# A spectral convolution with its mix of channels: the block-diagonal operand is loaded from DRAM instead of being spread on the engines

## The chip, the cores and the metric

The kernel runs on one core of a Trainium2 chip. The metric is the device time of one execution in microseconds, the median of three runs: 6919.16 us (6918.71 to 6933.95). The profile comes from one further execution with the profiler on.

A core has engines with queues of their own: PE (TensorE, matmuls; "PEld" is its loading of weights), DVE (VectorE), ACT (ScalarE), POOL (GpSimd) and SP (SyncE, which here only issues DMAs). They meet in semaphores. Data lies in SBUF (128 partitions), in PSUM (where matmuls write) and in DRAM. Sixteen DMA engines move data between DRAM and SBUF.

## The reference, cut to what matters

The input is `x[16, 16, 256, 256]` in float32 (batch, channel, y, x). Two layers follow one another, each on the group-normalised input and added to it. The change lies in the first, a Laplace-domain convolution:

```python
alpha = fft2(x)                                            # [b, i, o, x]
A  = 1 / (omega1[:, None, None, None] - weights_pole1)     # [o, i, k, p]
Bm = 1 / (omega2[:, None, None, None] - weights_pole2)     # [x, i, k, q]
S  = einsum('ikpq,oikp,xikq->oxik', weights_residue, A, Bm)
output_residue1 = einsum('biox,oxik->bkox', alpha, S)      # the mix
x1 = ifft2(output_residue1).real
# ... and a second term from the poles, x2; the layer adds x1 + x2/(256*256)
```

The **mix** is the second `einsum`: at each frequency (o, x) the 16 complex input channels `i` of each of 16 images are multiplied by a complex 16 x 16 matrix `S[o, x]`. The second layer (3 x 3 convolutions, an involution, a gate over channels) takes the greater part of the time and isn't touched.

## The kernel before

`forward` runs four parts one after another: `layer0_forward` (norm, Fourier transform, terms of the poles), `layer0_mix` (the mix and the inverse transform along x), `layer0_back` (inverse transform along y, sum, norm) and `layer1`. They hand over in DRAM: `layer0_forward` writes the spectrum to `al[33, 2, 64, 16, 256]`, with the indices group of four frequencies in y; real or imaginary part `v`; four frequencies `f` of the group times 16 channels; image; frequency in x. `layer0_mix` reads it and writes `hd`.

`layer0_mix` loops over 33 groups `g` of four frequencies in y (the last group has one that is used). For each group:

- `poles` (DVE) spreads the factors `A` of the group over a block-diagonal operand `lt`, three multiplies with the mask `m16`. The factors come by `load_poles` (line 579) into `av`, which has two buffers.
- `residues(lt, s, k0)`, called for k0 = 0, 2, ..., 14, builds the matrices `S` of the group: 16 matmuls with 32 columns of weights each (line 656) into PSUM, copied to `s[128, 256, 2, 16]` by ACT (line 667) or DVE (line 665).
- `mix(s, y, between)` does the multiplication: for each of 256 frequencies in x one matmul (line 679) with `s[:, i]` as weights (128 rows: four frequencies in y, times 16 channels, times real and imaginary; 32 columns) and `alb[:, i]` as the moving operand: 64 columns, that is 4 frequencies in y by 16 images. So that one matmul keeps the four frequencies apart, `alb` is block-diagonal: in column (j, b) only the 32 rows that belong to frequency j are not zero. Four matmuls in a row go to four different column groups of PE (`32 * q`). Sixteen of such fours fill a PSUM tile, and ACT copies it to `y` (line 686); there are four such quarters.
- `turn(y, f)` transposes on PE (line 695) and copies to `yt` by DVE (701) and ACT (699); `columns(g, f, yt)` does the inverse transform along x on PE (714), adds and subtracts on DVE (726, 727), and POOL issues four writes to `hd` (734). The `columns` of f = 3 runs in two halves between the quarters of the next mix (`between`).

The block-diagonal operand is made in two steps. `load_spectrum(g, q)` (SP, line 607) loads the images 4q to 4q + 3 of a group into `alc` (four buffers of 4 KB a partition) with four DMAs, one for each h, each of 128 KB; 16 for a group. `expand(t, q, j, eng)` then multiplies the tile by column j of the mask `m4` (one for rows of frequency j, zero elsewhere) and writes all of block j for these images: on ACT line 617, on DVE line 619. There are 16 such spreads a group, 6 on ACT and 10 on DVE, in the order of the table `spreads`.

The order of PE, ACT, DVE and POOL is written out by hand (`manual_schedule`); SP's is left to the scheduler. After `mix(g)` come residues for the next group, turn and columns for f = 0, 1, 2, a part of the spreads with each f, then the last spread, the last residues and turn for f = 3, and then `mix(g + 1)`. `alb` (64 KB a partition), `s`, `lt` and `y` have one buffer each. The spectrum that is spread in group g has been loaded during group g - 1.

The sides of a DMA have shapes that matter below. `load_spectrum` reads a pattern of 8 blocks x 4 rows x 1,024 words and writes 32 partitions x 1,024 words.

Of the kernel before, what the change touches and what calls it, by code (L numbers as in the profile page):

```python
# [10 lines left out]
F32 = mybir.dt.float32  # L11
I32 = mybir.dt.int32
AF = mybir.ActivationFunctionType
ALU = mybir.AluOpType
# [5 lines left out]
N = 256  # L20
G = 8
P = 128
NF = 33
# [33 lines left out]
def load(nc, pool, src, shape, name):  # L57
    t = pool.tile(shape, F32, tag=name, name=name)
    nc.sync.dma_start(out=t, in_=src)
    return t  # L60
# [505 lines left out]
def layer0_mix(ctx, tc, d, al, hd, tabs):  # L566
# [3 lines left out]
    nc = tc.nc  # L570
    nb = d["x"].shape[0]
    cp = ctx.enter_context(tc.tile_pool(name="mc", bufs=1))
    m16 = load(nc, cp, d["m16"], [P, 4], "m16")
# [3 lines left out]
    def load_poles(g):  # L577
        av = ap.tile([P, 32, 4, 3], F32, tag="av", name="av")
        nc.sync.dma_start(out=av.rearrange("p k f l -> p (k f l)"), in_=avd[g])
        return av  # L580

    av = load_poles(0)
# [6 lines left out]

    alb = cp.tile([P, N, 4, nb], F32, name="alb")
    m4 = load(nc, cp, d["m4"], [P, 4], "m4")

    lp = ctx.enter_context(tc.tile_pool(name="ml", bufs=1))
    gp = ctx.enter_context(tc.tile_pool(name="mg", bufs=1))
# [2 lines left out]
    pst = ctx.enter_context(tc.tile_pool(name="pst", bufs=2, space=PSUM))  # L599
    psh = ctx.enter_context(tc.tile_pool(name="psh", bufs=2, space=PSUM))  # L600

    def load_spectrum(g, q):

        t = gp.tile([P, 4, 2, P], F32, tag="alc", name="alc", bufs=4)
        src = al[g].rearrange("v (j h c) b x -> h (v j) c (b x)", h=4, c=4)
        for h in range(4):
            nc.sync.dma_start(
                out=t[32 * h : 32 * h + 32].rearrange("p b e x -> p (b e x)"),
                in_=src[h, :, :, 4 * q * N : 4 * q * N + 4 * N],
            )  # L610
        return t

    def expand(t, q, j, eng):

        dst = alb.rearrange("p (x e) j b -> p b e x j", e=2)[:, 4 * q : 4 * q + 4, :, :, j]
        if eng is nc.scalar:
            eng.activation(dst, t, AF.Copy, scale=m4[:, j : j + 1])
        else:
            eng.tensor_scalar(dst, t, m4[:, j : j + 1], None, ALU.mult)  # L619


    spreads = (
        (((0, 0), (1, 0)), ((0, 1), (0, 2), (0, 3))),
        (((1, 1), (2, 0)), ((1, 2), (1, 3), (2, 1))),
        (((3, 0), (3, 1)), ((2, 2), (2, 3), (3, 2))),
        ((), ((3, 3),)),
    )

    def spread(spectrum, f):
        for eng, parts in zip((nc.scalar, nc.vector), spreads[f]):  # L630
            for q, j in parts:
                expand(spectrum[q], q, j, eng)

    def poles(av):


        lt = lp.tile([P, 32, 3, 4, 4], F32, tag="lt", name="lt")
        shape = [P, 32, 4, 4]
        for plane in range(3):
            nc.vector.tensor_tensor(  # L640
                lt[:, :, plane],
                av[:, :, :, plane].unsqueeze(3).to_broadcast(shape),
                m16.unsqueeze(1).unsqueeze(2).to_broadcast(shape),
                ALU.mult,
            )
        return lt.rearrange("p (k g) l f c -> p k g l f c", g=4)

    def residues(lt, s, k0):

        kk = k0 // 2  # L650
        ps = psg.tile([P, 2, 2, N], F32, tag="pg", name="ps")
        for v in range(2):
            for g in range(4):
                for odd in range(2):
                    lanes = slice(64 * odd, 64 * odd + 64)
                    nc.tensor.matmul(
                        ps[32 * g : 32 * g + 32, odd, v],
                        lhsT=lt[lanes, kk, g, 1 - v : 3 - v].rearrange("p l f c -> p (l f c)"),
                        rhs=tt[lanes, kk, g],
                        start=True,  # L660
                        stop=True,
                    )
        dst, src = s[:, :, :, k0 : k0 + 2], ps.rearrange("p k v x -> p x v k")
        if kk % 2:
            nc.vector.tensor_copy(dst, src)
        else:
            nc.scalar.copy(dst, src)  # L667

    def mix(s, y, between):


        for x0 in range(0, 64, 16):
            if x0 >= 32:
                next(between, None)
            ps = psg.tile([P, 16, 64], F32, tag="pg", name="pg")
            for x in range(16):
                for q in range(4):
                    i = 4 * (x0 + x) + q
                    nc.tensor.matmul(  # L679
                        ps[32 * q : 32 * q + 32, x],  # L680
                        lhsT=s[:, i].rearrange("p v k -> p (v k)"),
                        rhs=alb[:, i].rearrange("p j b -> p (j b)"),
                        start=True,
                        stop=True,
                    )
            nc.scalar.copy(y[:, :, x0 : x0 + 16], ps.rearrange("p x j -> p j x"))

    def turn(y, f):

        yt = hp.tile([P, 8, 8, C], F32, tag="yt", name="yt", bufs=2)  # L690
        for t0 in range(0, 8, 4):
            pt = pst.tile([P, 4, P], F32, tag="pt", name="pt")
            for t in range(4):
                j = 16 * f + 2 * (t0 + t)
                nc.tensor.transpose(pt[:, t], y[:, j : j + 2].rearrange("p q x -> p (q x)"), ident)
            dst = yt[:, :, t0 : t0 + 4].rearrange("p c t k -> p t c k")
            src = pt.rearrange("p t (c k) -> p t c k", k=C)
            if t0:
                nc.scalar.copy(dst, src)
            else:  # L700
                nc.vector.tensor_copy(dst, src)  # L701
        return yt
# [35 lines left out]

    E = mybir.EngineType
    with tc.manual_schedule(engines={E.PE, E.Activation, E.DVE, E.Pool}):  # L740
        spectrum = [load_spectrum(0, q) for q in range(4)]
        lt = poles(av)
        av = load_poles(1)
        s = gp.tile([P, N, 2, C], F32, tag="s", name="s")
        for k0 in range(0, C, 2):
            residues(lt, s, k0)
        for q in range(4):
            spread(spectrum, q)
        for q in range(4):
            spectrum[q] = load_spectrum(1, q)  # L750
        between = iter(())
        for g in range(NF):
            more = g + 1 < NF
            y = gp.tile([P, 64, 64], F32, tag="y", name="y")
            if more:
                lt = poles(av)
            mix(s, y, between)
            if more:
                s = gp.tile([P, N, 2, C], F32, tag="s", name="s")
                residues(lt, s, 0)  # L760
            for f in range(4 if more else 1):
                if more and f == 3:
                    spread(spectrum, f)
                    for k0 in (12, 14):
                        residues(lt, s, k0)
                yt = turn(y, f)
                if more:
                    for k0 in range(2 if f == 0 else 4 * f, 4 * f + 4, 2) if f < 3 else ():
                        residues(lt, s, k0)
                    if f < 3:  # L770
                        spread(spectrum, f)
                    if g + 2 < NF:
                        if f == 0:
                            av = load_poles(g + 2)
                        spectrum[f] = load_spectrum(g + 2, f)
                between = columns(g, f, yt)
                if f < 3:
                    for _ in between:
                        pass
# [642 lines left out]
def fourier_tables():  # L1422

    k = np.arange(N)
# [3 lines left out]
    def parities(a):  # L1428
        return a.reshape(P, 2, *a.shape[1:])
# [12 lines left out]
        axis=1,  # L1442
# [13 lines left out]
    for t in tt:  # L1456
        for i in ii:
            mt[t, i, :, i // 4, t, i % 4] = 1
    out = {
        "fy": fy.reshape(P, 2, P),  # L1460
        "wx": parities(wx),
        "wxa": parities(wx[..., :P]),
        "wxn": wxn,
        "ix": ix,

        "iy": iy[..., :P].reshape(64, 2, 2, P).transpose(2, 0, 1, 3).reshape(P, 2, P),
        "ones": np.full((P, P), 1.0 / P),
# [7 lines left out]
        "sign_m": np.tile(np.repeat([-1.0, 1.0], 16), 4)[:, None],  # L1475
        "cm": np.tile(np.repeat(np.eye(2), 32, axis=0), (2, 1)),
        "mk": np.tile(np.repeat(np.eye(C), M, axis=0), (2, 1)),
        "m4": np.tile(np.repeat(np.eye(4), 4, axis=0), (8, 1)),
        "m16": np.tile(np.repeat(np.eye(4), M, axis=0), (8, 1)),
        "mt": mt.reshape(P, 4, 8),  # L1480
        "phase": np.repeat([0.25, 0.0], 64)[:, None],
# [73 lines left out]
```

## Time and profile before

| | us |
|---|---|
| median of 3 runs | 6919.16 |
| lowest, highest | 6918.71, 6933.95 |
| profiled execution, its own time | 6939.37 |
| its span, first to last instruction | 6937.6 |

| engine | busy us | share of the span |
|---|---|---|
| PE | 6375.2 | 92% |
| PEld | 3583.2 | 52% |
| DVE | 5451.1 | 79% |
| ACT | 3703.9 | 53% |
| POOL | 3635.8 | 52% |

A line of a group names the line of the kernel, the engine, the operation, the tile written and the tiles read, shapes and count; after the first bar stand busy time in us and the mean of one in ns, and after the second the idle time of the engine just before, with what ended it ("<-"). "issue" is waiting for nothing that the profile shows. In the timeline a line begins with start and length in us. In the tables of windows each engine's busy time stands with its count of instructions in brackets, then the granted clock of PE (1 is full), the mean busy share of the DMA engines and GB/s. Float32 matmuls are listed as two instructions each, so a mix of 256 matmuls shows 512. A matmul's own duration includes its way through the array; many overlap.

### The profile page before, as it was taken

Reading aid. Unit: us, or ns where it says so; the run is one execution under the profiler, and the core shown is the slowest. Engines: PE = TensorE matmul, PEld = TensorE weight load, DVE = VectorE, ACT = ScalarE, POOL = GpSimd, SP = SyncE. Lnnn points to the kernel's source line nnn. Section 1 sums busy time; section 2 is a strip of 40 time slices with the busy share of each in tenths; the row PEclk is TensorE's granted clock in tenths of the full one; section 3 lists DMA queues with packets and bytes.
Section 4 is the critical chain, followed back from the end, with each engine's and each line's share of the span. In section 5 each row is a group of like instructions: output and inputs, shape, how many; then the busy total and the mean of one; then the engine's idle time right before and its main releaser. Section 6 shows DMA issues by size and latency. Waiting matters only on the chain.

```text
span 6937.6 us, 153382 instructions
## 1 busy us (share of the span) xinstructions
PE 6375.2 (92%) x59944; PEld 3583.2 (52%) x59944; DVE 5451.1 (79%) x10057; ACT 3703.9 (53%) x5732; POOL 3635.8 (52%) x4614
## 2 busy tenths in 40 slices
PE   7899989978888888899789999999999999999996
PEld 5777777766766677677533333333333333333331
DVE  8888987356666666788788888888888888888885
ACT  1223333355655555222376666666666666666671
POOL 2334544523333333666665666666766566665563
PEclk9999999989999999999899999999999999999998
DMA  3444434433333333999877898888988889988886
GB/s 95 124 123 122 122 112 119 113 123 104 111 108 111 110 104 93 318 327 326 281 209 231 272 285 261 264 274 277 286 267 261 272 267 285 287 262 262 272 272 211
DMA packets 715941, 1443.97 MB, mean 208 GB/s; under 512 B 101338, under 2 KB 523542, under 8 KB 672950
## 3 DMA queue, kind: packets, MB, share of 16 engines
q1 hardware_dynamic: 567030, 959.77, 45.0%
q0 software_dynamic: 148192, 474.40, 21.8%
q8 instruction: 478, 7.83, 0.5%
q14 instruction: 241, 1.97, 0.1%
HBM read 877.12 MB, written 556.47 MB: 207 GB/s over the span
## 4 chain that ended last, share of the span: by engine, by line
PE 65%; DVE 20%; DMA 5%; issue 5%; ACT 4%; POOL 1%; SPq 0%; DVEq 0%; ACTq 0%; POOLq 0%
PE c2ps L1201 17%; PE c L1053 14%; PE pd L1121 13%; PE pg L679 4%; PE ph L714 3%; DVE alb L619 3%; ACT wide L1101 3%; PE px L313 2%; PE pu L207 2%; PE py L876 2%; PE pr L1080 2%; PE pv L214 2%; DVE u L224 2%; PE py L877 2%; DVE st L174 1%
## 5 line engine op out<-in xcount | busy, mean ns | idle before, releaser
L1101 ACT ACTIVATE wide<-c,b 32x512 f32<-32x512 f32 x2176 | 1479.6, 680 | 311.6 <-PE c L1053 263.5
L1132 DVE TENSOR_TENSOR top<-pd,t 32x512 f32<-32x512 f32 x2176 | 1504.0, 691 | 52.6
L1053 PE MATMUL c<-z,w 102*128 102x512 f32 x2048 | 999.7, 620 | 110.7 <-ACT wide L1101 89.3
L1113 POOL COPY wide<-wide 32x1031 f32<-32x1031 f32 (+1 forms) x576 | 579.7, 1006 | 881.5 <-ACT wide L1101 854.4
L1129 DVE TENSOR_TENSOR t<-pd,r 64x512 f32<-64x512 f32 x1088 | 744.1, 684 | 345.3 <-PE pd L1121 298.2
L1121 PE MATMUL pd<-wide,dw 128*128 128x512 f32 x2048 | 988.6, 604 | 12.0 <-DVE top L1132 11.0
L734 POOL DMA_DIRECT2D hd<-h x512 | 434.8, 856 | 955.0 <-DVE h L727 937.0
L1053 PEld LDWEIGHTS c<-z,w 102*128 102x128 f32 x2048 | 371.7, 192 | 697.5 <-issue 462.5
L1201 PE MATMUL c2ps<-rows,c 128*32 128x512 f32 x6144 | 721.6, 602 | 5.6 <-DVE odd L1228 5.6
L1121 PEld LDWEIGHTS pd<-wide,dw 128*128 128x128 f32 x2048 | 380.9, 192 | 572.2 <-issue 418.5
L1114 POOL COPY wide<-wide 32x1031 f32<-32x1031 f32 (+1 forms) x576 | 576.0, 1000 | 33.5
L1072 ACT ACTIVATE bot<-c,b 128x512 f32<-128x512 f32 x544 | 344.4, 684 | 462.6 <-issue 381.4
L714 PE MATMUL ph<-ix,yt 64*128 64x256 f32 x4128 | 507.9, 394 | 17.6 <-DVE yt L701 14.7
L313 PE MATMUL px<-wxn,u 128*64 128x256 f32 x4224 | 481.5, 379 | 2.4 <-ACT o L320 2.4
L207 PE MATMUL pu<-fy,eo 128*128 128x128 f32 x2048 | 436.2, 297 | 42.0 <-DVE u L224 35.2
L714 PEld LDWEIGHTS ph<-ix,yt 64*128 64x128 f32 x4128 | 419.6, 192 | 89.9 <-ACT s L667 29.6
L679 PE MATMUL pg<-alb,s 128*32 128x64 f32 x16896 | 311.6, 237 | 154.1 <-issue 71.8
L1201 PEld LDWEIGHTS c2ps<-rows,c 128*32 128x32 f32 x6144 | 174.8, 108 | 513.5 <-issue 404.5
L889 POOL TENSOR_TENSOR x<-x,o 128x512 f32<-128x512 f32 x256 | 324.4, 1267 | 217.3 <-DVE o L888 197.5
L619 DVE TENSOR_SCALAR alb<-alc,m 128x1024 f32<-128x1024 f32 x330 | 424.1, 1415 | 0.0
L214 PE MATMUL pv<-at,eo 128*128 128x128 f32 x2048 | 423.0, 291 | 0.0
L726 DVE TENSOR_TENSOR h<-ph,odd 128x256 f32<-128x256 f32 x258 | 113.4, 440 | 389.4 <-ACT odd L723 389.4
(221 smaller groups left out, 11460.2 us busy)
## 6 DMA issues: line engine op xcount, KB each, us to landing
rows<-cf SPq DMA_DIRECT2D x128, 2176.0 KB
z<-zn SPq DMA_DIRECT2D x768, 257.8 KB
cf<-top POOLq DMA_DIRECT2D x512, 240.0 KB, 6.9
cf<-bot POOLq DMA_DIRECT2D x96, 840.0 KB, 10.8
alc<-al SPq DMA_DIRECT2D x528, 128.0 KB
zn<-zb SPq DMA_DIRECT2D x128, 516.0 KB
o<-zn SPq DMA_DIRECT2D x128, 516.0 KB
z<-in_x SPq DMA_DIRECT2D x64, 1024.0 KB
```

The source lines that it names most:

```text
L313: nc.tensor.matmul(ps[64 * k : 64 * k + 64, :, h], lhsT=u[:, h, part, g0 + j + k].rearrange("p f c -> p (f c)"), rhs=wxn[:, h, part], star ...
L619: eng.tensor_scalar(dst, t, m4[:, j : j + 1], None, ALU.mult)
L679: nc.tensor.matmul(ps[32 * q : 32 * q + 32, x], lhsT=s[:, i].rearrange("p v k -> p (v k)"), rhs=alb[:, i].rearrange("p j b -> p (j b)"), s ...
L714: nc.tensor.matmul(ph[q][:, e], lhsT=yt[lanes, i].rearrange("p t k -> p (t k)"), rhs=ix[lanes, i], start=n == 0, stop=n == 3,)
L1053: nc.tensor.matmul(ps[:, a], lhsT=w, rhs=z[:k, c : c + 2, 0:N], start=True, stop=True)
L1101: nc.scalar.activation(self.feat[64 - 32 * q : 96 - 32 * q, f, self.groups[g], :H], ps[q][32 * f : 32 * f + 32], AF.Mish, bias=b1[0][32 * ...
L1113: nc.gpsimd.tensor_copy(flat[0:32, f, 1:m], flat[64:96, f, 0 : m - 1])
L1114: nc.gpsimd.tensor_copy(flat[96:128, f, 0 : m - 1], flat[32:64, f, 1:m])
L1121: nc.tensor.matmul(ps, lhsT=dwt if self.tail else dw, rhs=self.feat[:, f, cs, :H], start=True, stop=True,)
L1129: nc.vector.tensor_tensor(t[64:128], ps[:64], self.r[:, cs], ALU.mult)
L1132: nc.vector.tensor_tensor(self.top[32 * f : 32 * f + 32, cs, q], ps[lanes], t[lanes], ALU.add)
L1201: nc.tensor.matmul(ps[32 * j : 32 * j + 32], lhsT=w[:, blk], rhs=src[:, 4 * j + blk : 4 * j + blk + 4, x : x + H], start=(i, blk) == (0, 0 ...
```

## The change

`alc`, `expand`, the mask `m4` and the table `spreads` go. `alb` is laid out with the frequency in x innermost and set to zero once; each group's spectrum is loaded by 16 DMAs straight into the diagonal blocks (8 partitions x 16 KB each), after the mix of the group before. The rows of the contraction get another order for that (h, f, v, c instead of h, v, f, c), so `poles` builds `lt` in that order, in two multiplies instead of three. The moving operand of the mix takes one frequency out of `spectra`, whose columns are 256 words apart; before they were next to one another.

```diff
-    alb = cp.tile([P, N, 4, nb], F32, name="alb")
-    m4 = load(nc, cp, d["m4"], [P, 4], "m4")
+    alb = cp.tile([P, 4, nb, N], F32, name="alb")
+    nc.vector.memset(alb[:, :2], 0.0)
+    nc.gpsimd.memset(alb[:, 2:], 0.0)
+    spectra = alb.rearrange("p f b x -> p (f b) x")
...
-    def load_spectrum(g, q):
-
-        t = gp.tile([P, 4, 2, P], F32, tag="alc", name="alc", bufs=4)
-        src = al[g].rearrange("v (j h c) b x -> h (v j) c (b x)", h=4, c=4)
-        for h in range(4):
-            nc.sync.dma_start(
-                out=t[32 * h : 32 * h + 32].rearrange("p b e x -> p (b e x)"),
-                in_=src[h, :, :, 4 * q * N : 4 * q * N + 4 * N],
-            )
-        return t
-
-    def expand(t, q, j, eng):
...
-    def spread(spectrum, f):
...
+    def load_spectrum(g):
+
+        src = al[g].rearrange("v (f h c) b x -> h f v c (b x)", f=4, h=4)
+        for f in range(4):
+            for h in range(4):
+                lanes = slice(32 * h + 8 * f, 32 * h + 8 * f + 8)
+                nc.sync.dma_start(
+                    out=alb[lanes, f].rearrange("p b x -> p (b x)"), in_=src[h, f]
+                )
...
-        lt = lp.tile([P, 32, 3, 4, 4], F32, tag="lt", name="lt")
-        shape = [P, 32, 4, 4]
-        for plane in range(3):
+        lt = lp.tile([P, 2, 32, 4, 2, 4], F32, tag="lt", name="lt")
+        shape = [P, 128, 2, 4]
+        for v in range(2):
...
-                        lhsT=lt[lanes, kk, g, 1 - v : 3 - v].rearrange("p l f c -> p (l f c)"),
+                        lhsT=lt[lanes, v, kk, g],
...
-                        rhs=alb[:, i].rearrange("p j b -> p (j b)"),
+                        rhs=spectra[:, :, N // 2 * (i % 2) + i // 2],
...
-        spectrum = [load_spectrum(0, q) for q in range(4)]
+        load_spectrum(0)
...
             mix(s, y, between)
             if more:
+                load_spectrum(g + 1)
                 s = gp.tile([P, N, 2, C], F32, tag="s", name="s")
                 residues(lt, s, 0)
             for f in range(4 if more else 1):
                 if more and f == 3:
-                    spread(spectrum, f)
                     for k0 in (12, 14):
                         residues(lt, s, k0)
...
-                    if f < 3:
-                        spread(spectrum, f)
-                    if g + 2 < NF:
-                        if f == 0:
-                            av = load_poles(g + 2)
-                        spectrum[f] = load_spectrum(g + 2, f)
+                    if f == 0 and g + 2 < NF:
+                        av = load_poles(g + 2)
```

## Prediction

> **What bounds the kernel now.** I read the page's slices first: the mix is the stretch of slices 8 to 16 (1,380 to 2,770 us), where DMA is busy 3 to 4 tenths and PE 8 to 9. Then I took the mix alone. The costliest groups between 1,412 and 2,770 us (busy, mean ns, idle before) hold the two that the change removes:
>
> ```profile
> L619 DVE TENSOR_SCALAR alb<-alc,m 128x1024 f32<-128x1024 f32 x321 | 413.6, 1416 | 0.0
> L617 ACT ACTIVATE alb<-alc,m 128x1024 f32<-128x1024 f32 x192 | 376.2, 2060 | 0.0
> L679 PE MATMUL pg<-alb,s 128*32 128x64 f32 x16896 | 311.6, 237 | 154.1 <-issue 71.8 <-DVE s L665 68.7 <-DMA alc<-al 13.2
> ...
> L686 ACT COPY y<-pg 128x1024 f32<-128x1024 f32 x132 | 133.7, 1013 | 422.4 <-PE pg L679 422.4
> ```
>
> DVE is busy 850 of these 1,358 us, ACT 786, PE 1,188: PE sets the pace, and the spreads touch it only through the 68.7 us before L679. The timeline of one group shows how:
>
> ```profile
> 1943.66 19.00 SPq L607 DMA_DIRECT2D alc<-al  x16
> ...
> 1958.43 1.45 DVE L619 TENSOR_SCALAR alb<-alc,m 128x1024 f32<-128x1024 f32 x1
> ...
> 1959.70 1.19 DVE L665 COPY s<-ps 128x1024 f32<-128x1024 f32 x1
> ...
> 1961.04 2.95 PE L679 MATMUL pg<-alb,s 128*32 128x64 f32 x195 [2.15 <-DVE s L665]
> ...
> 1972.13 1.99 PE L679 MATMUL pg<-alb,s 128*32 128x64 f32 x128
> ...
> 1975.99 1.99 PE L679 MATMUL pg<-alb,s 128*32 128x64 f32 x128
> ```
>
> The 16 loads are issued under the work between two mixes, a whole group ahead; the last spread ends just before the mix, and PE waits 2.15 us. Reading the first and last L679 start of all 33 groups off the timeline: a mix lasts 15.8 us in the mean (13.3 to 19.5), the next starts 26.1 us after it ends (25.7 to 27.6). The work between the mixes, in windows (PE, PEld, DVE, ACT, POOL busy, granted clock, DMA share):
>
> ```profile
> 1935.30:1961.00 25.70, 22.97 (x384) 17.49 (x384) 22.82 (x30) 20.75 (x21) 13.06 (x16) 1.00 0.42 124
> 1961.00:1978.00 17.00, 13.29 (x552) 11.71 (x560) 3.71 (x8) 3.68 (x5) 0.61 (x2) 0.90 0.26 79
> ```
>
> So a group is 15.8 + 26.1 us, and PE works 23.0 of the 26.1.
>
> **What goes.** 330 DVE spreads of 1,415 ns and 198 ACT spreads of 2,059 ns: 467 and 408 us of engine time. On the path is only what PE waits for: 26.1 us cannot fall below PE's 23.0, so at most 3.1 us a group; I take 2.5, because turn and the s copies keep their own waits: 33 x 2.5 = 82 us. `poles` goes from three multiplies of 688 ns to two of twice the size (1,220 ns each, by the 1,024-element copy L665): 2.1 to 2.4 us on a DVE idle during the mix, nothing. The memsets of alb write 8,192 words a partition: 4,128 words took POOL 3.5 us, so about 7 us, once, while the first loads wait for the last writes of al anyway; without that cover 7 us.
>
> **What comes in: the load on the path.** alb is one buffer. Built, the first load of a group waits for the last matmul of the mix, and the first matmul of the next mix waits for all 16 loads; nothing is loaded ahead any more. The load must fit into the 23 to 26 us between mixes, or PE waits for the rest. Behind the waiting SP instruction only the other 15 loads queue (the `av` load for two groups on is ahead of them), so nobody else waits for that.
>
> How long do 2 MB take? Before, a load of 128 KB is 8 source blocks into 32 partitions. While such loads run back to back (1,396 to 1,404 us) the packet records show exactly 8 packets of queue 1 in flight for 68% of the time and more for 9%: eight engines, the same eight for each load. The trace also says why eight. An engine that finishes its part leaves one 4-byte packet. Queue 1 has 36,538 of them; 1,024 are one-word data rows; the other 35,514 are exactly the sum over all SP loads of the largest number up to 16 that divides the outermost counts of both sides: 16 for most, 10 and 3 for the `z` windows of 10 and 3 rows, 8 for `alc`. The new load is `src[h, f]` (v 2, c 4, 4,096 words) into 8 partitions. The outermost counts are 2 and 8: **two engines**, by the above the same two for all 16 loads.
>
> - Bytes: 1 MB per engine. A 4 KB packet took 159 ns, the 16.5 KB ones 615 ns at best; rows are now 16 KB: 64 x 0.61 = 39.1 us (40.7 if cut into 4 KB).
> - Beside it, on the same engines: the 16 `hd` writes of a group, 2 MB over 16 engines if spread evenly, 32 x 0.159 = 5.1 us; `av`, 8 x 0.065 = 0.5 us.
> - Start: SP's issue at 1,986.49, first packet at 1,987.92: 1.4 us.
>
> Sum 46.1 us, from 40.8 (no collision) to 49 (4 KB packets and a slow wake-up). The 26.1 us become 46.1: +20.0 a group, and the 2.5 us gained are swallowed. The first group pays the same: its loads leave at about 1,390 and two engines end near 1,432, where the mix began at 1,412.6. 33 x 20.0 = **+660 us**.
>
> [...]
>
> **A colder PE.** PE then idles 20 us before each mix. The first group shows what that does:
>
> ```profile
> 1395.00:1412.00 17.00, 3.29 (x109) 1.67 (x96) 14.49 (x13) 13.38 (x8) 0.00 (x0) 0.67 0.52 189
> 1412.00:1420.00 8.00, 5.66 (x202) 5.45 (x206) 2.06 (x4) 1.01 (x1) 0.00 (x0) 0.50 0.50 171
> ```
>
> After 13 us of idle the clock stood at 0.50 for the first 9 us. That mix took 16.15 us without the two interposed halves of `columns` (2.08 us each) that the others hold: 15.8 - 4.2 = 11.6, so +4.5 us. Bounds 0 (the stalls of "issue" inside the mix, 1 to 4 us, are filled while PE waits) and 5. 32 x 4.5 = **+144 us**.
>
> **Columns innermost.** The mix's moving operand went from 64 consecutive words to 64 words 1 KB apart. No matmul of the trace with more than two columns has such an operand; the price is bounded. Below: nothing. Above: the four column groups overlap now (a quarter of the mix is 64 matmuls, listed as 128 halves: 1.99 us, 31 ns a matmul, where one half alone takes 219); if they came to read one after another, 4 x 1.99 us a quarter, 8 to 32 us a mix, and the clock would no longer matter: +20 to +24. The nearest rows: ACT's spread writes words 512 B apart at 2,060 ns where L686, same size, needs 1,013, a factor 2; DVE's L224, which reads words 256 B apart, needs 587 ns for 256 words where L726 needs 440, a factor 1.3. I take 2, on the half of the mix that runs warm (at half clock PE asks for words half as fast): 2 x 1.99 = +4 us, 33 x 4 = **+132 us**. [...]
>
> **Sum.** The profiled execution took 6,939.4 us (span 6,937.6), 20 above the median of 6,919.2. 6,939 + 660 + 144 + 132 = 7,875; less 20: **7,855 us**. About 0.3% either way, 21 us, is what a measurement of this kernel can tell from no change.
>
> **Rivals.**
> - *Two engines, and the strided columns serialise PE.* (20.0 + 22) x 33 = 1,386: about 8,285, from 8,220. For: all four concurrent columns now start within 516 bytes of each other and step by a power of two. Against: no row shows a factor above 2. 24%.
> - *Faster: the load spreads.* If 16 loads ran on eight engines, 2 MB take 256 KB/26 GB/s = 10 us, 14 as issued today, hidden under 23 us; the 82 us are kept: 6,838. It decides at four engines (19.6 + 1.4 + 3 = 24 us). It needs the completion count above to be accident, and free columns. 5%.
> - *The load spreads, but the columns cost a factor 2 or so* on an always warm mix, about +4 us a group after stalls: 6,838 + 130 = 6,970, with the first rival's price far more. 3%. Between this and the last, within 0.3%: 2%.
>
> **How the numbers follow.** The forecast, two engines with a stride factor between 1 and 2, has 66%: without stride cost 7,723; with the load at 42 us, no cold clock and no stride 6,919 + 33 x 16 = 7,450; with load 49 and both costs 7,955. The serial rival adds up to 8,300. The range of 7,530 to 8,260 leaves out the faster and even cases (8%), the lowest corner of the forecast (4%) and the top of the serial case (8%). Faster 5%, same 2%, slower 93%.
>
> **What would show it.** Right: the mix's first matmul waits some 20 us for "DMA alb<-al" in each group; queue 1 loses 528 x 6 completion packets; the gap between mixes is 44 to 49 us; DVE and ACT lose 467 and 408 us with no gain; clock 0.5 at each mix's start. Cold and stride show in the mix's length: 20 us with columns free, 24 with a factor 2, over 35 if serial. Wrong: gaps of 23 to 26 us (load hidden), or a PE wait that ends on something else.

## The result and the profile after

The changed kernel takes 8140.27 us (median of 4 runs, 8129.30 to 8148.91) where the kernel before takes 6920.35 (4 runs): the ratio is 1.176 [1.174, 1.178]. The profiled execution took 8141.01, its span is 8139.2.

The page of the changed kernel, engine totals and two groups:

```profile
PE 6923.2 (85%) x59944; PEld 4103.9 (50%) x59944; DVE 5192.0 (64%) x9695; ACT 3427.3 (42%) x5534; POOL 3506.3 (43%) x4615
...
L659 PE MATMUL pg<-alb,s 128*32 128x64 f32 x16896 | 893.7, 403 | 828.9 <-DMA av<-avd 481.1
...
L666 ACT COPY y<-pg 128x1024 f32<-128x1024 f32 x132 | 136.1, 1031 | 1576.6 <-PE pg L659 1576.6
```

L659 is the mix's matmul, L679 before. Two numbers grew. Its busy time went from 311.6 to 893.7 us with the same 16,896 instructions, and the idle time ahead of it from 154 to 829. ACT has its spreads no longer and waits 1,577 us for PE at the copy of `y`. The waits of the same kernel (total, times, longest) split the 829:

```profile
PE pg L659 <- DMA av<-avd: 481.1, 19, 36.9
...
PE pg L659 <- DMA alb<-al: 347.8, 14, 25.5
```

19 and 14 make 33: in every group the mix waits, 25.1 us in the mean. The first matmul waits for several loads at once. In 19 groups the small `av` load, which SP issues last, carries the name; in all 33 the last 16 KB packet of `alb` ends 0.5 to 1.1 us before the mix starts. The timeline of one group:

```profile
1941.65 11.74 SPq L610 DMA_DIRECT2D alb<-al  x5
...
1955.78 0.32 SPq L579 DMA_DIRECT2D av<-avd  x1
...
1975.66 14.04 PE L659 MATMUL pg<-alb,s 128*32 128x64 f32 x256 [24.24 <-DMA av<-avd]
...
1991.56 6.86 PE L659 MATMUL pg<-alb,s 128*32 128x64 f32 x128
...
2000.28 7.01 PE L659 MATMUL pg<-alb,s 128*32 128x64 f32 x128
...
2007.36 3.18 SPq L610 DMA_DIRECT2D alb<-al  x5
```

The reader is to see three things. PE stands still for 24.24 us. A quarter of the mix (128 listed halves) takes 6.9 to 7.0 us where it took 1.99. And the loads for the next group are issued at 2,007.36, as the mix ends. The same group in windows, the mix and then the stretch to the next one (PE, PEld, DVE, ACT, POOL busy, clock, DMA share, GB/s):

```profile
1975.60:2007.30 31.70, 31.64 (x552) 29.42 (x560) 4.11 (x4) 6.43 (x5) 1.25 (x2) 0.94 0.02 4
2007.30:2055.50 48.20, 22.83 (x385) 16.84 (x386) 13.90 (x22) 9.44 (x15) 8.27 (x14) 0.78 0.27 92
```

In the second, PE works 22.83 of 48.2 us, the same work as before in 25.7.

Over all 33 groups, a mix taken from the start of its first matmul to the end of its last (the 15.8 and 26.1 us of the prediction are taken so too):

| | mix, us | to the next mix, us |
|---|---|---|
| before | 15.82 | 26.08 |
| after | 30.68 | 47.70 |

The stretches between give (47.70 - 26.08) x 32 = 692 us, the mixes (30.68 - 15.82) x 33 = 490, and the first mix starts 19 us later. The sum is 1,201; the spans differ by 1,201.6. So nothing else pays: some three fifths of the loss are the load, less what the missing spreads give back between the mixes, and two fifths are the longer mixes, which the experiments put down to the columns.

### The profile page after: what moved, and what is told of

Same layout as the page of the kernel before. It is cut to its first block, busy times and chain, and to the rows that moved or that the text cites. A ratio compares the mean times of both kernels' runs of the same rounds, so it can differ in the third digit from the quotient of the medians.

```text
span 8139.2 us, 152351 instructions
## 1 busy us (share of the span) xinstructions
PE 6923.2 (85%) x59944; PEld 4103.9 (50%) x59944; DVE 5192.0 (64%) x9695; ACT 3427.3 (42%) x5534; POOL 3506.3 (43%) x4615
## 5 line engine op out<-in xcount | busy, mean ns | idle before, releaser
L659 PE MATMUL pg<-alb,s 128*32 128x64 f32 x16896 | 893.7, 403 | 828.9 <-DMA av<-avd 481.1
L706 DVE TENSOR_TENSOR h<-ph,odd 128x256 f32<-128x256 f32 x258 | 183.1, 710 | 1807.8 <-ACT odd L703 1793.4
L714 POOL DMA_DIRECT2D hd<-h x512 | 304.2, 600 | 2284.9 <-DVE h L707 2229.3
L659 PEld LDWEIGHTS pg<-alb,s 128*32 128x32 f32 x16896 | 849.9, 152 | 865.7 <-issue 857.2
L666 ACT COPY y<-pg 128x1024 f32<-128x1024 f32 x132 | 136.1, 1031 | 1576.6 <-PE pg L659 1576.6
L694 PE MATMUL ph<-ix,yt 64*128 64x256 f32 x4128 | 489.1, 384 | 0.7 <-ACT yt L679 0.7
L694 PEld LDWEIGHTS ph<-ix,yt 64*128 64x128 f32 x4128 | 386.2, 187 | 98.3 <-issue 45.8
```

The lines of the kernel that those rows point to most:

```text
L659: nc.tensor.matmul(ps[32 * q : 32 * q + 32, x], lhsT=s[:, i].rearrange("p v k -> p (v k)"), rhs=spectra[:, :, N // 2 * (i % 2) + i // 2], ...
L694: nc.tensor.matmul(ph[q][:, e], lhsT=yt[lanes, i].rearrange("p t k -> p (t k)"), rhs=ix[lanes, i], start=n == 0, stop=n == 3,)
```

## Experiments on the load

**e1_side_by_side**: the loads of the changed kernel, but the mix reads 64 neighbouring words.

```diff
-                        rhs=spectra[:, :, N // 2 * (i % 2) + i // 2],
+                        rhs=alb.rearrange("p f b x -> p (f b x)")[:, 64 * i : 64 * i + 64],
```

> The changed kernel, but the mix reads 64 words that lie next to one another (at 64 i of the same buffer) instead of 64 words 1 KB apart; what it multiplies is then not the right columns. The loads stay as they are, on two engines, with the wait in front of each mix. Theory 'stride': the words 1 KB apart take the overlap of the four column groups away; then the mix falls from 30.7 us to between 15.8 and 20 (the 20 if the clock of 0.50 after the wait costs 4.5 us), the gap between mixes stays 46 to 48 us, and the time is 7,650 to 7,790 us. Rival 'cold PE': the mix is long because PE has idled 20 us; then it stays near 30 us and the time near 8,140.

Measured: 7053.20 us, ratio 1.019 [1.017, 1.022]; mix 21.8 us, to the next 23.8. The expectations missed, because the edit changed more than the step. A matmul now touches one block f only, so each quarter waits for its own four loads, and a block is loaded again as soon as its quarter is done. The loads move under the mix. A stretch of loads and the quarter beside it in the timeline:

```profile
1962.53 28.89 SPq L610 DMA_DIRECT2D alb<-al  x12
1968.17 3.64 PE L659 MATMUL pg<-alb,s 128*32 128x64 f32 x128 [5.67 <-DMA alb<-al]
```

PE waits 5.67 us within the mix and SP issues beside it. The run still says something: a group takes 21.8 + 23.8 = 45.6 us, which is as long as two engines need for a group's load (45.1 us in the changed kernel). Even overlapped all round, that load stands above the 41.9 us of a group before.

**e2_eight_engines**: the spectrum in DRAM gets `v` innermost of the four (`al[33, 64, 2, 16, 256]`), so that the source's outermost count is 8; `lt` follows. **e3_both** adds the edit of e1.

```diff
-    al = dram.tile([NF, 2, 64, nb, N], F32, name="al")
+    al = dram.tile([NF, 64, 2, nb, N], F32, name="al")
...
-        src = al[g].rearrange("v (f h c) b x -> h f v c (b x)", f=4, h=4)
+        src = al[g].rearrange("(f h c) v b x -> h f (c v) (b x)", f=4, h=4)
```

> The changed kernel with another order in DRAM: real and imaginary part lie next to each other for each channel, so that a load reads 8 rows one after another into its 8 partitions, outermost counts 8 and 8 instead of 2 and 8; poles builds its operand in the matching order. The result is complete. Theory 'two engines': a load now runs on eight engines, 2 MB take 10 us and some 16 with the issue, hidden under PE's 23 to 24 us; the gap between mixes falls from 47.7 to 23.5 to 26, queue 1 shows 8 packets in flight, the mix stays 27 to 31 us, and the time is 7,350 to 7,420. Rival 'single buffer': the wait is that of any load which may start only when the mix has ended, whatever its engines; then the gap stays above 40 us and the time above 7,900.

> The two edits of the runs before together: loads on eight engines, and a mix that reads 64 words next to one another (not the right columns). If two engines and the stride are the whole of the loss, this is what taking the spreads off the engines is worth: mix 15 to 16.5 us, gap 23 to 24.5, time 6,830 to 6,900, that is 0.3 to 1.2% below the kernel before. If there is a third cost (the larger lt, the order of the queues, a load that still ends late) it stays above 6,940.

Measured: e2 7763.06 us, 1.122 [1.120, 1.124], mix 30.9, to the next 35.5; e3 7197.32, 1.041 [1.039, 1.043]. The 35.5 us lie between the theory (26 at most) and the rival (above 40), and e3 shows the third cost that its expectation left room for. In e2 the packet records mostly show eight packets of 16 KB in flight, four times the two of the changed kernel, but each takes 1,713 ns (median of all; the expectation of e4 has 1,658) instead of 614. From its first packet to its last, the load of a group takes 33.1 us in the mean (2 MB, 63 GB/s) instead of 45.1. Eight engines cut it by a quarter, not to a quarter. The waits of e2 between 1,432 and 3,580 us show who else pays:

```profile
POOL hd L714 <- DMA hd<-h: 452.6, 111, 10.2
...
DVE h L706 <- DMA hd<-h: 331.2, 45, 10.5
...
PE pg L659 <- DMA alb<-al: 200.8, 19, 14.5
```

POOL and DVE wait for the writes to `hd`. Whether these writes queue behind the slow packets on the same engines isn't shown: the records don't name a packet's engine, and the 4 KB packets of the writes themselves are little longer (252 ns in the mean against 209 in the changed kernel). e3 shares e1's finer waits and can't be compared with e2 alone; that it is slower than e1 (7,197 against 7,053) fits, since its packets took 2,034 ns.

**e4_ports**: e2, with the eight destination partitions of each load 12 apart instead of neighbours. The same source, bytes, count of engines and rows; rows of the operand land in other partitions.

```diff
-                lanes = slice(32 * h + 8 * f, 32 * h + 8 * f + 8)
+                lanes = slice(h, h + 85, 12)
```

> The kernel of e2_eight_engines (loads on eight engines, time 7,763, gap between mixes 35.5 us, one 16 KB packet 1,658 ns instead of 614 on two engines), but each load writes 8 partitions that lie 12 apart instead of 8 side by side; the rows then lie in the wrong lanes. Source, bytes, engines and count of DMAs are the same. Theory 'landing': 8 neighbouring partitions are written no faster than two engines can fill them, so eight engines share the same 60 GB/s; spread out, a packet goes back to 610 to 900 ns, a group's load to 11 to 18 us, the gap to 23.5 to 27, time 7,380 to 7,480. Rival 'source': eight engines that read 128 KB of DRAM in a row get in each other's way there; then packets stay near 1,650 ns and the time near 7,760.

Measured: 7334.81 us (one run; before on that chip 6932.98); to the next mix 23.4 us. Both lie just below what was expected. Packets fell to 611 ns and a group's load to 14.7 us (143 GB/s). The timeline:

```profile
1967.09 12.45 SPq L610 DMA_DIRECT2D alb<-al  x16
...
1990.38 13.14 PE L659 MATMUL pg<-alb,s 128*32 128x64 f32 x256 [0.41 <-issue]
```

All 16 loads are issued in 12.45 us after the mix, PE works through, and waits 0.41 us at the next mix for nothing that the profile shows. The source is the same, so what held e2 is the landing in eight neighbouring partitions. That is a second limit of this load, behind the two engines: 63 GB/s into neighbours, 143 into partitions 12 apart.

## Experiments on the columns

**s256_before_strided**: the kernel before, spreads and loads untouched, with a moving operand whose 64 words lie 256 words (1,024 B) apart. Then one run each with other steps S: 2, 4 and 252 words.

```diff
+                    at = 128 * (i % 2) + i // 2
...
-                        rhs=alb[:, i].rearrange("p j b -> p (j b)"),
+                        rhs=alb.rearrange("p x j b -> p (x j b)")[:, at : at + 63 * S + 1 : S],
```

(For S of 2 and 4, `at` is chosen so that successive matmuls of one column group share a stretch of 64 S words, and the four concurrent ones lie in four quarters of the buffer. For 252 and 256 `at` is the same, and the four start within 516 bytes of each other, as in the changed kernel.)

> The kernel before, with its spreads and its loads a group ahead, but the mix reads 64 words 1 KB apart out of alb, at the places the changed kernel uses (so not the right columns). PE does not idle here. Theory 'stride': a quarter of the mix takes 6.5 to 7 us instead of 2.0, the mix 29 to 32 us, the gap stays 26, time 7,390 to 7,470. Rival 'cold PE': the mix stays near 16 us and the time at 6,920 to 6,960.

> The kernel before, but the mix reads every second word (8 bytes apart), the four concurrent matmuls in different quarters of the buffer; not the right columns. s256_before_strided, with words 1 KB apart, had a mix of 31.4 us instead of 15.8. Theory 'line': what counts is how many useful words lie in 16 bytes; 2 of 4 give a factor of about 2 on the 2.0 us of a quarter, the mix is 21 to 25 us, time 7,090 to 7,240. Rival 'bank': only steps by a large power of two collide; then the mix stays 15.8 and the time 6,920 to 6,960.

> As s2_stride_2, with every fourth word (16 bytes apart). Theory 'line': one useful word in 16 bytes, as at 1 KB, so the full price: quarters of 6.5 to 7 us, mix 30 to 32 us, time 7,410 to 7,460. Rival 'bank': mix 15.8 us, time 6,920 to 6,960.

> As s256_before_strided, with words 252 apart (1,008 bytes) instead of 256 (1,024 bytes). Theory 'line': no difference, mix 30 to 32 us, time 7,410 to 7,460. Rival 'bank' (steps by a power of two fall on the same part of the memory): mix well below, 16 to 24 us, time 6,930 to 7,200.

| step | mix, us | to the next | time, us | before on that chip |
|---|---|---|---|---|
| 256 words | 31.41 | 25.75 | 7431.86 | 6918.09 |
| 252 | 19.97 | 25.76 | 7064.81 | 6932.98 |
| 4 | 19.62 | 25.76 | 7045.21 | 6932.98 |
| 2 | 15.65 | 25.94 | 6927.60 | 6932.98 |

The ratio of the 256-word run is 1.074 [1.072, 1.076]; the others are single runs, but the lengths are means over 33 mixes. The 256-word run came out as theory 'stride' had it; of the other three, 252 and 2 words met their rival 'bank', and 4 words met neither side. A late quarter of the mix in each timeline, steps 256, 252, 4 and 2 in this order:

```profile
3012.25 7.04 PE L681 MATMUL pg<-alb,s 128*32 128x64 f32 x128
```

```profile
2791.07 3.99 PE L681 MATMUL pg<-alb,s 128*32 128x64 f32 x128
```

```profile
2773.35 3.92 PE L681 MATMUL pg<-alb,s 128*32 128x64 f32 x128
```

```profile
2712.43 2.11 PE L681 MATMUL pg<-alb,s 128*32 128x64 f32 x128
```

Against 1.99 us for neighbours: a step of 8 bytes costs next to nothing (2.11), 16 bytes a factor 2 (3.92), and 1,008 bytes hardly more than 16 (3.99). Of the steps tried, only 1,024 bytes cost 3.5 (7.04). So two prices were measured: the factor 2 of the prediction at 16 and 1,008 bytes, and another 1.8 at 1,024. With 1,024 B a matmul takes 7.04 / 64 = 110 ns instead of 31. Four column groups taking turns would need 4 x 1.99 = 7.96 us a quarter by the prediction's bound, 13% more than measured; the runs don't tell taking turns from slower reads in all four. Nor was a step of 1,024 B run with the four concurrent columns far apart, so how much their closeness has to do with the 1.8 is open.

The strided run has PE busy throughout, no load on the path, and the mix of the changed kernel: 31.4 against 30.7 us. The columns alone cost (31.41 - 15.82) x 33 = 514 us.

**e5_no_later_loads**: the changed kernel without the loads of later groups, so that every mix uses the first group's spectrum.

```diff
             if more:
-                load_spectrum(g + 1)
```

> The changed kernel, but only the first group's spectrum is loaded; the later groups mix that one again. Nothing then waits for a load, PE does not idle before a mix, and the spreads are gone. If the load is the whole of the longer gap and the idle clock costs nothing beside the stride: gap 23.5 to 24.5 us, mix 30 to 31.5, time 7,330 to 7,400, some 80 below s256_before_strided (7,432), which has the stride and the spreads. If the cold clock had its 4.5 us in the changed kernel's mix of 30.7 us, the mix would be 26 us here and the time near 7,200.

Measured: 7353.03 us, 1.062 [1.060, 1.065]; mix 30.60, to the next 23.39. A window over one mix:

```profile
1975.00:2007.00 32.00, 31.89 (x534) 27.71 (x526) 8.19 (x7) 10.28 (x9) 2.36 (x4) 1.00 0.09 25
```

The clock is 1.00 here and 0.94 in the changed kernel's mix, and the mix is no shorter: 30.60 against 30.68 us. In the changed kernel the cold clock is there, but brief:

```profile
1975.60:1983.00 7.40, 7.33 (x135) 7.36 (x139) 0.00 (x0) 0.00 (x0) 0.00 (x0) 0.74 0.02 4
1983.00:1991.50 8.50, 8.50 (x145) 7.63 (x137) 0.00 (x0) 2.02 (x2) 0.00 (x0) 1.00 0.01 2
```

Over the 33 mixes the clock stands at 0.50 for the first 1.7 to 5.0 us, 3.4 in the mean. A PE that is cold for so long costs nothing beside these columns. With the load gone and the columns kept, 787 of the 1,220 us are gone; e4, which loads everything, only faster, ends at the same time (7,335): a load that fits into the gap costs nothing.

**What the strided reads do to others.** Line 640 (DVE multiplies of `lt`) of the strided run, duration minimum, median and maximum in ns, and then the same line of the kernel before:

```profile
L640 DVE TENSOR_TENSOR lt<-av,m x99: 684/2572/6408, 1373.5 to 3174.6; 128x512 f32<-128x512 f32 x99
```

```profile
L640 DVE TENSOR_TENSOR lt<-av,m x99: 670/686/723, 1380.9 to 2716.6; 128x512 f32<-128x512 f32 x99
```

And the ACT copy of the interposed columns in the changed kernel:

```profile
L703 ACT COPY odd<-ph x258: 372/378/3647, 1465.5 to 3977.4; 128x256 f32<-128x256 f32 x129
```

The median is unharmed, because 194 of the 258 run between mixes; the 64 beside a mix all take 1.57 to 3.65 us (at 2,000.42 two took 3.39 together). With steps of 2, 4 and 252 words line 640 keeps its time (medians of 0.69, 0.68 and 0.68 us, 0.78 at most). The copy of `y` keeps its 1.01 us even beside the strided run's matmuls, so it isn't every access; what sets the slowed ones apart was not tested.

## What the spreads were worth

**e6_before_no_spread** leaves both `spread` calls out of the loop of the kernel before. **e7_spread_on_pool** moves the last spread of a group from DVE to POOL.

```diff
-        ((), ((3, 3),)),
+        ((), ()),
...
+        if f == 2:
+            expand(spectrum[3], 3, 3, nc.gpsimd)
```

> The kernel before without its spreads after the first group (alb keeps the first group's spectrum; the loads into alc go on). This is what the engine work that the change removes is worth on the path: PE's waits for ACT and DVE between two mixes are 3.1 us of 26.1; the prediction took 2.5 us a group, 82 us: gap 23.5 to 24, time 6,820 to 6,860. If PE's waits have other causes (turn, the copies of s), the gap stays near 26 and the time within 0.3% of 6,918.

> The kernel before, complete, with the last of the 16 spreads of a group (images 12 to 15, frequency 3) moved from DVE, where it stands between the last columns and the last copy of s, to POOL one step earlier. PE's wait of 2.15 us for that copy in front of each mix should shrink by the spread's 1.4 us: 32 x 1.4 = 45 us, time 6,870 to 6,880. Rival: POOL holds DVE or its own writes of hd up (it issues 16 of them a group), or its spread ends later than DVE's did: no change or slower, 6,915 to 6,960.

Measured: e6 6832.99 us, 0.988 [0.986, 0.990], 92 us less; e7 6943.25, 1.0035 [1.0023, 1.0046]. The mix's matmul in the groups of e6 between 1,412 and 2,670 us:

```profile
L679 PE MATMUL pg<-alb,s 128*32 128x64 f32 x16581 | 274.6, 223 | 91.1 <-issue 76.0 <-DVE s L665 14.6
```

The wait for the `s` copy has shrunk from 68.7 to 14.6 us, which leaves half a microsecond a group. e7 in the timeline:

```profile
1952.86 4.88 DVE L619 TENSOR_SCALAR alb<-alc,m 128x1024 f32<-128x1024 f32 x3
1952.93 6.61 POOL L619 TENSOR_SCALAR alb<-alc,m 128x1024 f32<-128x1024 f32 x1
...
1960.25 2.95 PE L681 MATMUL pg<-alb,s 128*32 128x64 f32 x195 [1.97 <-DVE s L667]
```

POOL needs 6.61 us for one spread, beside it DVE's three take 4.88, and PE waits 1.97 us as it did 2.15. The spread left DVE and the wait stayed: over all groups PE waits 77.2 us for the `s` copy (68.7 before), and beside that its weight loads wait 73.8 us, in 28 groups, for POOL's spread. DVE's slowest spread takes 5.09 us where the slowest before took 1.49; why was not tested.

**e8_spread_in_mix** keeps the operand and the load of before and moves spreads to where DVE and ACT are idle: into the mix. After each of the first three quarters the columns just used are free, and 8, 8 and 2 of the group's 32 half spreads go there (`within`); 14 stay between the mixes. The spectrum is in half tiles, `h` has four buffers instead of five for the space.

```diff
-    def expand(t, q, j, eng):
+    def expand(spectrum, k, j, half, eng):
+        part = slice(32 * k, 32 * k + 32)
+        src = spectrum[half][:, :, :, part]
...
+            if spectrum is not None:
+                spread(spectrum, within[x0 // 16])
```

> The kernel before, complete, with its spreads cut by quarters of the mix instead of by images: as soon as a quarter of the mix has read its 64 columns, the spreads of the next group for these columns may run, under the rest of the mix, where DVE and ACT have some 13 us of idle time a group. 18 of now 32 half-sized spreads run there, 14 between the mixes as before; the loaded spectrum lies in three half buffers. If the spreads cost what e6_before_no_spread shows (92 us, 1.3%), and the engine time between the mixes is what they cost it with, most of that comes back: gap 23.5 to 24.5 us, mix 15.5 to 16.5, time 6,835 to 6,880. Rival: the spreads under the mix hold the copies of y and the last columns up, or slow PE's reads of the same buffer; then the mix grows by more than the 2 us that the gap gives back, and the time is 6,920 to 6,990.

Measured: 6862.34 us (5 runs, 6852.86 to 6865.39; before there 6925.16), 0.991 [0.990, 0.992]. It is faster than both kernels. The timeline of one mix:

```profile
1960.33 2.43 PE L691 MATMUL pg<-alb,s 128*32 128x64 f32 x159 [0.46 <-DVE s L677]
...
1962.49 3.09 DVE L624 TENSOR_SCALAR alb<-alc,m 128x512 f32<-128x512 f32 x6
1963.29 2.07 ACT L622 ACTIVATE alb<-alc,m 128x512 f32<-128x512 f32 x2
...
1969.19 3.13 DVE L624 TENSOR_SCALAR alb<-alc,m 128x512 f32<-128x512 f32 x6 [3.60 <-PE pg L691]
```

PE waits 0.46 us for the `s` copy, six spreads of DVE follow a quarter's end, and the way to the next mix falls from 26.08 to 23.73 us with the mix at 15.95. Two thirds of what e6 shows to be there come back, without the load.

## Why the prediction was right or wrong

- **The load on the path** was right in mechanism, rate and size. Two engines: two packets of 16 KB in flight, more for only 2 of some 1,450 us, each 614 ns (taken: 0.61). From mix to mix 47.7 us (taken: 46.1; bounds 40.8 to 49). 660 us were predicted, 692 + 19 measured. The completion counts fell from 36,538 to 33,354, which is 528 x 6 and 16 for the load of the mask.
- **The 82 us of the spreads** are real (92 in e6) and were swallowed, as said. In e6 they don't lie between the mixes alone (23.9 us to the next mix against 26.1): the mix is shorter too (14.9 against 15.8). DVE's and ACT's totals fell by 259 and 277 us only, not by 467 and 408: what ran beside the mix became slower (the adds and subtractions into `h` by 122 us in all, DVE's L726, now L706, from 440 to 710 ns in the mean; the copies to `odd` on ACT by 114). That gave no time either way.
- **The columns** were the term that was mis-sized: +4 us a mix were taken (132 us), by a factor 2 on the half that runs warm. Measured alone they cost 15.6 a mix in the strided run. The step that failed is "I take 2, on the half of the mix that runs warm": the factor 2 is what steps of 4 and 252 words cost (3.92 and 3.99 us a quarter against 1.99), but a step of 1,024 bytes costs 3.5 (7.04), on all quarters of the mix, warm or not (in the changed kernel 6.95, 6.36, 7.06 and 7.05 us in the mean), nearer the 4 of the serial rival. No row of the profile before could show it. The rival's "step by a power of two" was right to fear this step, but it doesn't mark it off: 8 and 16 bytes are powers of two as well and cost next to nothing and a factor 2.
- **The colder PE** was taken at +144 us and cost nothing (e5: 30.60 against 30.68 us). The clock was cold, as foreseen, but for 3.4 us of a mix and not for the 9 that the first group had shown, and the columns set the pace; the prediction had itself written that under a serial read the clock would no longer matter. Together the two terms were +4.5 and +4 us a mix against +14.9 measured.
- **The total** lies 285 us above the forecast: 214 from the mixes, 51 from the load, and the 20 that were taken off for the profiled execution, which this time (8,141) lies at the median. The forecast's own highest corner was 7,955; that 8,140 lies inside the range is owed to the room that was left for the serial rival. (That rival's sum, (20.0 + 22) x 33 on 6,919, gives 8,305, not 8,285.)
- **"It decides at four engines"**, in the rival of the hidden load, was wrong as a condition: with eight engines into eight neighbouring partitions the load still takes 33.1 us (e2). With partitions that lie apart, eight engines hide it (14.7 us in e4); four were not tried. The 26 GB/s an engine in that rival are the 4 KB in 159 ns of the profile before.

Left open: why 1,024 B differs from 1,008, and which of ACT's and DVE's accesses it slows; e1 and e3 can't separate the load from the finer waits. A second `alb`, which would let the loads go ahead, wasn't tried; it would take another 64 KB a partition.

## What to carry to other kernels

In these runs a DMA was priced by where it landed as well as by how many engines carried it: eight rows of 16 KB into neighbouring partitions came at 63 GB/s with eight engines, into partitions 12 apart at 143. Before an operand is laid out for a load's convenience, price the step with which a matmul will read it, and try a step other than 1,024 bytes: here 8 bytes left the mix at 15.7 us, 16 and 1,008 bytes had it at some 20 and 1,024 at 31. And work that seems to be on the wrong engine may only be at the wrong time: moved into the stretch where its engines idle, the spreads gave 0.9%.

## What was not expected of the hardware

- A moving operand with a step of 1,024 B slows ACT and DVE beside it, up to 3.65 us for a copy of 0.38 and 6.4 for a multiply of 0.69. Beside steps of 8, 16 and 1,008 B the multiply takes 0.78 at most, and beside 16 and 1,008 B the copy 0.46.
- A 16 KB packet took 614 ns on each of two engines, 1,713 on each of eight into eight neighbouring partitions as well, and 611 on each of eight into partitions 12 apart.
- A step of two words in the moving operand was free (2.1 us a quarter against 1.99).
